# Attention output projection of head pairs: seven products of half blocks in place of eight, summed over the heads in SBUF

## Chip, core and metric

The kernel runs on one core of one Trainium2 chip. The metric is the device time of the whole program in microseconds (us), as the median of several runs. A profile is one further execution, recorded by the hardware; its span goes from the first to the last instruction.

## What is computed

One pre-norm transformer block on x of 1 x 1024 x 512, all in f32: x + attention(layernorm(x)), then that plus a feed-forward part of its own layernorm. The feed-forward part has three 512 x 512 matrices of signs and two ReLUs. The attention has 32 heads of 128 (keys) and 128 (values):

```python
q = einsum('bsd,de->bse', hidden, wq).reshape(B, S, H, DQ)[..., :DN]
k, v = ...                      # from hidden @ wkv, per head 128 and 128
scores = einsum('bqhd,bkhd->bhqk', q, k) * DQ ** -0.5      # causal mask
attn = einsum('bhqk,bkhd->bqhd', softmax(scores), v).reshape(B, S, H * DV)
return einsum('bse,ed->bsd', attn, wo)                     # wo: 4096 x 512
```

The change concerns the last line, the output projection: 1024 tokens x 4096 by 4096 x 512, summed over all heads.

## The kernel before, in words

Heads go in 16 pairs (G = 2). At the start x is loaded as eight tiles of 128 tokens (L76 to 79), normalised, and transposed into `xnT` (4 chunks of 128 features x 1024 tokens, L201).

**Projections q, k, v of a pair** (`products`, L260) are already done by a Strassen scheme: the operands are cut in two along the features, the two heads and the two token halves, and seven products are formed in place of eight. `token_sums` (L215) makes the token-side sums once; `weight_sums` (L227) makes four weight-side sums of 128 x 256 for each projection and pair, on GpSimd. The function yields after each product, so that the loop below can mix products with other work.

**The loop** (L441) walks over 32 heads x 8 tiles of 128 queries: 16 steps a pair, `s` = 0 to 15. A step issues

- the loads and weight sums due at this step (weights of the next pair),
- `probabilities` of the next step (L354): the score matmul into the only score buffer (`ps_sc`, two banks of PSUM), VectorE's mask-and-minimum (L369), ScalarE's exponential (L380), VectorE's reciprocal (L384), ScalarE's scaling (L385), and a VectorE transpose in blocks of 32 x 32 into `tb` (L387),
- one or two products of the chain v of this pair, q and k of the next one,
- at eight of the steps, `o_unit` (L342) of the *previous* pair: the output projection of one tile of 128 tokens, two matmuls of 512 columns (one for each head) into one PSUM bank, and a VectorE add of that bank to the tile of x (L352),
- after each fourth tile of queries, `exchange` (L391): 16 or 32 DMAs of 64 KB on SyncE's queue (SP), which finish the transposition from `tb` into `pT`,
- four steps after an exchange, `attend` (L407): probabilities times values for 512 queries, and a VectorE copy into `attnT` (L423).

A bank of PSUM takes one tile of 128 x 512 here; `ps_mm` has three banks, shared by the attention outputs and the projection, and `ps_st` three for the chain.

**The order of the work.** The program text gives the order in which instructions come up; when the program is built, a planner lays down a fixed order for each engine and each queue, in text order among the instructions whose inputs and buffers it expects to be there. On the chip each engine runs its list in order and waits where it must. A tile name with `bufs=n` has n buffers that are reused in turn.

**The end.** After the loop the last attend runs (L480), then for each tile of tokens the last pair's `o_unit` (L506), the second layernorm, a transposition, and a split into a coarse and a fine part. Three layers of matmuls follow (L520 twice, L545), and the final add takes the tile of x again (L553). The sign matrices are loaded in the last head's first step (L471) into buffers of weights that are free by then (L160).

Of the kernel before, what the change touches and what calls it, by code (L numbers as in the profile page):

```python
# [13 lines left out]
P = 128  # L14
# [5 lines left out]
G = 2  # L20
# [9 lines left out]
def kernel(  # L30
# [44 lines left out]
    xs = []  # L75
    for t in range(NT):  # L76
        xt = const.tile([P, D], F32, tag=f"x{t}", name=f"x{t}")
        nc.sync.dma_start(xt, x_v[:, t, :])
        xs.append(xt)
# [30 lines left out]
    def load_qk_weights(which, g):  # L110
        w = pairs.tile([P, G, NC, DN], F32, tag="wraw", name=f"w{'qk'[which]}{g}", bufs=3)
# [9 lines left out]
    def load_v_weights(g):  # L121
        wv_sb[g] = pairs.tile([P, NC, G * DV], F32, tag="wv", name=f"wv{g}")
        first = H * DN + g * G * DV
        nc.sync.dma_start(wv_sb[g], wkv_v[:, :, first : first + G * DV])
# [7 lines left out]
    load_v_weights(0)  # L132
    load_qk_weights(0, 1)
    load_o_weights(0)
# [25 lines left out]
    def sign_weights(i, k, slots):  # L160
# [4 lines left out]
        chunks = []  # L165
        for c in range(NC):
            if c % 2 == 0:
                pl, tag = slots[c // 2]
                w = pl.tile(
                    [P, 2, D], F32R, tag=tag, name=f"w{i}_{c}", bufs=3 if tag == "wraw" else None  # L170
                )
# [6 lines left out]
            nc.gpsimd.tensor_scalar(w[:, c % 2, :], kt[:, c, :], mul, add, ALU.mult, ALU.add)  # L178
            chunks.append(w[:, c % 2, :])
        return chunks  # L180

    def normalise(t, name):
        stats = small.tile([P, 6], F32, tag="stats", name=f"stats_{name}{t}")
        nc.vector.bn_stats(stats, xs[t])
# [7 lines left out]
        nc.vector.tensor_scalar(xn, xs[t], mv[:, 0:1], rstd, ALU.subtract, ALU.mult)  # L192
# [9 lines left out]
    for t in range(NT):  # L202
        nc.scalar.copy(xnT[:, :, t * P : (t + 1) * P], transposed(t, normalise(t, "a"), "a"))
# [22 lines left out]

    def weight_sums(which, g):  # L227
        s = pairs.tile([P, 4, 2, DN], F32, tag="wsum", name=f"wsum{'qkv'[which]}{g}")

        def A_(i, j):  # L230
            return A(which, g, i, j)

        nc.gpsimd.tensor_tensor(s[:, 0], A_(1, 0), A_(1, 1), ALU.add)  # L233
        nc.gpsimd.tensor_tensor(s[:, 1], s[:, 0], A_(0, 0), ALU.subtract)
        nc.gpsimd.tensor_tensor(s[:, 2], A_(0, 0), A_(1, 0), ALU.subtract)
        nc.gpsimd.tensor_tensor(s[:, 3], A_(0, 1), s[:, 1], ALU.subtract)
        w_sum[which, g] = s

    qT, kT, vs, attnT = {}, {}, {}, {}
# [20 lines left out]
    def products(which, g):  # L260
# [5 lines left out]
        if which == 2:  # L266
            d = []
            for h in (g * G, g * G + 1):
                vs[h] = heads.tile([P, NT, DV], F32, tag="v", name=f"v{h}")
                d.append([vs[h][:, k * TPB : (k + 1) * TPB, :] for k in range(NQB)])  # L270
# [49 lines left out]
        product(Y, s[:, 1], T[1], True, False)  # L320
# [6 lines left out]
        product(Y, s[:, 2], T[2], False, False)  # L327
# [4 lines left out]
        product(Z, s[:, 0], T[0], True, False)  # L332
# [5 lines left out]
        product(Z, s[:, 3], B(1, 1), False, True)  # L338
        plus(d[0][1], Z, u2)
        yield  # L340

    def o_unit(g, t):  # L342
        ps = ps_mm.tile([P, D], F32, tag="mm", name=f"ps_o{g}_{t}")
        for j in range(G):
            nc.tensor.matmul(  # L345
                ps,
                lhsT=attnT[g * G + j][:, t * P : (t + 1) * P],
# [59 lines left out]
    def attend(h, qb, pieces):  # L407
        g, j = divmod(h, G)
        if qb == 0:
            attnT[h] = heads.tile([P, S], F32, tag="attnT", name=f"attnT{h}")  # L410
# [11 lines left out]
        dst = attnT[h][:, qb * QB : (qb + 1) * QB]  # L422
        nc.vector.tensor_copy(dst.rearrange("p (t a i) -> p a t i", a=NB, i=B32), ps)  # L423

# [16 lines left out]
    for i, (h, qt) in enumerate(steps):  # L441
        g, j = divmod(h, G)
        s = NT * j + qt
        if s == 0:
            if g > 0:
                load_o_weights(g)
# [4 lines left out]
        if s == 5 and g + 1 < NG:  # L451
            weight_sums(1, g + 1)
            load_v_weights(g + 1)
# [9 lines left out]
        o_steps = (2, 4, 6, 8, 10, 12, 14, 15)  # L463
# [131 lines left out]
```

## Time and profile before

| what | value |
|---|---|
| median of 3 runs (lowest, highest) | 1413.53 us (1410.81, 1413.58) |
| the profiled execution's own time | 1412.72 us |
| its span | 1410.9 us |
| granted TensorE clock, mean | 0.989 |
| busy: TensorE matmul, VectorE, ScalarE, GpSimd | 1372.4, 733.1, 490.0, 153.8 us |
| output projection, matmul records (L345) | 512, busy 240.9 us |
| its VectorE adds (L352) | 128, 87.8 us busy, 686 ns each |
| DMAs of the exchange (L400) | 1536, median 2.0 us from issue to landing |

A matmul of f32 appears as two records and two weight loads in the profile, so 512 records are 256 matmuls. A group of instructions is shown as line, engine, operation, output<-input, shape, count, then its busy time, the mean of one, and the engine's idle time before them with what ended it. "Idle before" is time in which that engine waited for its next instruction's inputs; on an engine that is not the bottleneck it costs nothing. The chain of work is followed back from the last instruction to what released each piece. In a timeline each row has start, length, engine, line, operation, and in brackets the idle time before it.

### The profile page before, as it was taken

To read this page: it belongs to the slowest core of one execution; us is meant where nothing else is said; L and a number is where in the kernel's file an instruction comes from. 1 tells how busy PE (TensorE), PEld (TensorE's weight loads), DVE (VectorE), ACT (ScalarE), POOL (GpSimd) and SP (SyncE) were. 2 spreads that over 40 slices of the span, in tenths; PEclk is the share of its full clock that TensorE was granted. 3 is DMA by queue.
4 is the path that set the end of the run, shared out by engine and by line. 5 is a ranking of instruction groups with operands and counts; after the bars stand their busy time and mean duration, and the time that the engine had idled before them with its cause. 6 is when DMAs were issued, how large, how long until landed. Compare 5 with 4: busy or idle time off the path is not lost.

```text
span 1410.9 us, 15526 instructions
## 1 busy us (share of the span) xinstructions
PE 1372.4 (97%) x5000; PEld 791.6 (56%) x5000; DVE 733.1 (52%) x1561; ACT 490.0 (35%) x919; POOL 153.8 (11%) x213
## 2 busy tenths in 40 slices
PE   7999999999999999999999999999999999998598
PEld 4656464655646465554646455464645556463257
DVE  3455455555555555555455555544555554454275
ACT  2434333333333333333433333333333333333131
POOL 5110001010010101001010100100010110000200
PEclk9999999999999999999999999999999999998799
DMA  5234435353543435354443435344353434333401
GB/s 179 60 88 100 100 72 131 82 127 82 131 99 99 114 74 126 84 127 102 105 105 78 125 86 124 96 114 101 81 127 83 125 88 119 88 88 93 108 6 60
DMA packets 272176, 140.30 MB, mean 99 GB/s; under 512 B 26848, under 2 KB 265952, under 8 KB 272096
## 3 DMA queue, kind: packets, MB, share of 16 engines
q1 hardware_dynamic: 272096, 139.31, 39.7%
q8 instruction: 41, 0.67, 0.2%
q14 instruction: 39, 0.32, 0.1%
HBM read 36.44 MB, written 2.10 MB: 27 GB/s over the span
## 4 chain that ended last, share of the span: by engine, by line
PE 96%; DVE 2%; SPq 1%; DMA 1%; ACT 0%; issue 0%; DVEq 0%
PE sc L359 18%; PE ps_av L415 18%; PE ps_o L345 15%; PE Y_v L299 6%; PE Y_q L289 5%; PE Y_k L289 5%; PE X_v L299 4%; PE Z_v L299 4%; PE X_k L289 4%; PE X_q L289 4%; PE Z_k L289 4%; PE Z_q L289 4%; PE ps_h L520 2%; PE ps_out L545 1%; PE ps_q L255 1%; PE ps_k L255 1%
## 5 line engine op out<-in xcount | busy, mean ns | idle before, releaser
L380 ACT ACTIVATE p<-p,nmax 128x128 f32<-128x128 f32 (+7 forms) x256 | 198.0, 773 | 633.0 <-DVE nmax L369 625.8
L359 PE MATMUL sc<-kT,qT 128*128 128x512 f32 (+3 forms) x768 | 296.6, 491 | 7.0 <-DVE nmax L369 7.0
L415 PE MATMUL ps_av<-pT,v 128*128 128x512 f32 (+3 forms) x768 | 270.0, 495 | 14.6 <-DMA pT<-tb 14.6
L369 DVE CUSTOM_DVE_ANT_0 p<-sc,mask 128x128 f32<-128x128 f32 (+7 forms) x256 | 192.3, 751 | 153.6 <-PE sc L359 153.3
L345 PE MATMUL ps_o<-wo,attnT 128*128 128x512 f32 x512 | 240.9, 593 | 0.0
L415 PEld LDWEIGHTS ps_av<-pT,v 128*128 128x128 f32 x768 | 147.1, 194 | 150.1 <-issue 126.6
L359 PEld LDWEIGHTS sc<-kT,qT 128*128 128x128 f32 x768 | 140.4, 191 | 157.7 <-issue 142.9
L385 ACT ACTIVATE p<-p,rtotal 128x128 f32<-128x128 f32 (+7 forms) x256 | 194.5, 770 | 74.4 <-DVE rtotal L384 74.3
L387 DVE STREAM_TRANSPOSE tb<-p 128x128 f32<-128x128 f32 (+7 forms) x256 | 183.8, 755 | 12.3 <-ACT p L385 8.8
L352 DVE TENSOR_TENSOR x<-x,ps_o 128x512 f32<-128x512 f32 x128 | 87.8, 686 | 121.4 <-PE ps_o L345 121.2
L345 PEld LDWEIGHTS ps_o<-wo,attnT 128*128 128x128 f32 x512 | 92.1, 190 | 90.1 <-issue 87.8
L384 DVE RECIPROCAL rtotal<-total 128x1 f32<-128x1 f32 x256 | 40.5, 159 | 132.6 <-ACT p L380 132.5
L423 DVE COPY attnT<-ps_av 128x512 f32<-128x512 f32 x64 | 43.8, 684 | 55.2 <-PE ps_av L415 55.2
L233 POOL TENSOR_TENSOR wsumk<-wk 128x256 f32<-128x256 f32 x15 | 10.9, 726 | 491.6 <-DMA wk<-in_L_attn_wkv_dram 441.4
L299 PE MATMUL X_v<-wv,xnT 128*128 128x128 f32 x512 | 63.2, 275 | 0.0
L299 PEld LDWEIGHTS X_v<-wv,xnT 128*128 128x128 f32 x512 | 61.4, 192 | 1.3 <-issue 0.5
L289 PE MATMUL X_k<-xnT,wk 128*128 128x512 f32 x120 | 57.1, 592 | 0.0
L289 PE MATMUL X_q<-xnT,wq 128*128 128x512 f32 x120 | 57.1, 592 | 0.0
L233 POOL TENSOR_TENSOR wsumq<-wq 128x256 f32<-128x256 f32 x15 | 10.9, 726 | 339.1 <-PE Z_k L289 312.3
L380 ACT ACTIVATION_READ_ACCUMULATOR p<-p,nmax 128x1 f32 x256 | 47.8, 187 | 0.0
L312 DVE TENSOR_TENSOR v<-Z_v,u_v 128x512 f32<-128x512 f32 x32 | 22.1, 692 | 49.4 <-PE Z_v L299 49.4
L312 DVE TENSOR_TENSOR kT<-Z_k,u_k 128x512 f32<-128x512 f32 x30 | 20.6, 688 | 33.9 <-PE Z_k L289 33.9
(118 smaller groups left out, 1347.6 us busy)
## 6 DMA issues: line engine op xcount, KB each, us to landing
pT<-tb SPq DMA_DIRECT2D x1536, 64.0 KB, 2.0
wq<-in_L_attn_wq_dram SPq DMA_DIRECT2D x32, 256.0 KB, 3.3
wk<-in_L_attn_wkv_dram SPq DMA_DIRECT2D x32, 256.0 KB, 4.4
wv<-in_L_attn_wkv_dram SPq DMA_DIRECT2D x16, 512.0 KB, 4.1
wo<-in_L_attn_wo_dram SPq DMA_DIRECT2D x16, 512.0 KB, 4.0
x<-_attn_hidden_states_dram SPq DMA_DIRECT2D x8, 256.0 KB, 5.1
out_dram<-osb SPq DMA_DIRECT2D x8, 256.0 KB, 2.0
k<-in_L_ffn_k_dram SPq DMA_DIRECT2D x3, 256.0 KB, 3.4
```

The source lines that it names most:

```text
L289: nc.tensor.matmul(ps, lhsT=a[:, c, :], rhs=b[:, c, :], start=start, stop=stop, skip_group_check=True,)
L299: nc.tensor.matmul(ps[:, t, :], lhsT=b[:, c, t * P : (t + 1) * P], rhs=a[:, c, :], start=start and t == 0, stop=stop and t == TPB - 1, ski ...
L312: nc.vector.tensor_tensor(out, ps, other, ALU.add)
L345: nc.tensor.matmul(ps, lhsT=attnT[g * G + j][:, t * P : (t + 1) * P], rhs=wo_sb[g][:, j, :], start=(j == 0), stop=(j == G - 1),)
L352: nc.vector.tensor_tensor(xs[t], xs[t], ps, ALU.add)
L359: nc.tensor.matmul(sc[:, cols], lhsT=qT[h][:, qt * P : (qt + 1) * P], rhs=kT[h][:, cols], start=True, stop=True,)
L369: nc.vector.tensor_tensor_reduce(out=p[:, :n], in0=sc[:, :n], in1=mask[:, S - n :], scale=1.0, scalar=BIG, op0=ALU.add, op1=ALU.min, accum ...
L380: nc.scalar.activation(p[:, :n], p[:, :n], AF.Exp, bias=nmax, scale=-1.0, accum_out=total)
L385: nc.scalar.activation(p[:, :n], p[:, :n], AF.Copy, scale=rtotal)
L387: nc.vector.transpose(tb[qb][:, : qt + 1, :, i, :], p[:, :n].rearrange("p (c b k) -> p c b k", b=NB, k=B32))
L415: nc.tensor.matmul(ps[:, :, first:, :], lhsT=vs[h][:, kc, :], rhs=pieces[kc // TPB][:, kc % TPB, :, first:, :], start=(kc == 0), stop=(kc ...
L423: nc.vector.tensor_copy(dst.rearrange("p (t a i) -> p a t i", a=NB, i=B32), ps)
```

## The change

For each pair of heads, take the attention output as a 2 x 2 block matrix (two halves of 512 tokens by two heads) and wo's 256 rows as one (two heads by two halves of 256 output columns). The same scheme of seven products then gives the projection of a pair; each product is 512 tokens x 128 by 128 x 256, four matmuls of 256 columns.

- `o_products` (new) forms them. Each product is done in two halves of two token tiles, so that a half fills one PSUM bank; VectorE adds the half to `acc`, a tile of 7 x 4 x 256 per partition that keeps each *product* summed over the pairs (a copy for the first pair). The loop takes one half in every step from 2 to 15.
- `sums_of` (new) makes the weight-side sums on GpSimd, now in three new tiles and one in place, for q, k, v and wo alike. `attn_sums` (new) makes the four sums of attention outputs on GpSimd, one after the even head's second block and three after the odd head's.
- `add_products` (new) runs once, after the loop: eleven VectorE adds of 128 x 1024 combine the seven sums into x.
- The last pair keeps `o_unit`.
- To make room, x is loaded into the tile that becomes `acc`, and loaded again near the end into that of `xnT`. The weights of q and k have 2 buffers for 3, those of v 1 for 2, v itself 3 for 4; the attention outputs have one tile for each head of a pair and each half of the tokens. The load of wo goes from step 0 to step 6. The sign matrices and the hidden layers use other buffers.

The diff, cut to its core:

```diff
+    x_in = load_x("acc", "x_in")
...
     load_v_weights(0)
+    load_o_weights(0)
     load_qk_weights(0, 1)
-    load_o_weights(0)
...
+    def sums_of(a, tag, name, bufs):
+        t = pairs.tile([P, 3] + list(a(0, 0).shape[1:]), F32, tag=tag, name=name, bufs=bufs)
+        nc.gpsimd.tensor_tensor(t[:, 0], a(1, 0), a(1, 1), ALU.add)
+        nc.gpsimd.tensor_tensor(t[:, 1], t[:, 0], a(0, 0), ALU.subtract)
+        nc.gpsimd.tensor_tensor(t[:, 2], a(0, 1), t[:, 1], ALU.subtract)
+        nc.gpsimd.tensor_tensor(a(1, 0), a(0, 0), a(1, 0), ALU.subtract)
+        return [t[:, 0], t[:, 1], a(1, 0), t[:, 2]]
...
+    def attn_sums(g, early):
...
+        if early:
+            t0 = new(0)
+            nc.gpsimd.tensor_tensor(t0, b(0, 1), b(0, 0), ALU.subtract)
+            a_sum[g] = [t0]
+            return
+        t0, t1, t3 = a_sum[g][0], new(1), new(3)
+        nc.gpsimd.tensor_tensor(b(0, 1), b(1, 1), b(0, 1), ALU.subtract)
+        nc.gpsimd.tensor_tensor(t1, b(1, 1), t0, ALU.subtract)
+        nc.gpsimd.tensor_tensor(t3, b(1, 0), t1, ALU.subtract)
+        a_sum[g] = [t0, t1, b(0, 1), t3]
...
+        for m, left, right in (
+            (0, lambda: attn[g * G, 0], a(0, 0)),
+            (1, lambda: attn[g * G + 1, 0], a(0, 1)),
+            (2, lambda: a_sum[g][2], s[2]),
+            (3, lambda: a_sum[g][0], s[0]),
+            (4, lambda: a_sum[g][1], s[1]),
+            (5, lambda: a_sum[g][3], a(1, 1)),
+            (6, lambda: attn[g * G + 1, 1], s[3]),
+        ):
+            left = left()
+            for half in range(2):
+                ps = ps_mm.tile([P, 2, DH], F32, tag="mm", name=f"ps_o{g}_{m}_{half}")
+                for i in range(2):
+                    tok = slice((2 * half + i) * P, (2 * half + i + 1) * P)
+                    nc.tensor.matmul(
+                        ps[:, i, :], lhsT=left[:, tok], rhs=right, start=True, stop=True
+                    )
+                dst = acc[:, m, 2 * half : 2 * half + 2, :]
+                if g == 0:
+                    nc.vector.tensor_copy(dst, ps)
+                else:
+                    nc.vector.tensor_tensor(dst, dst, ps, ALU.add)
+                yield
...
+    def add_products(xt):
+        def to(d, k, m):
+            dst = xt[:, k * TPB : (k + 1) * TPB, d * DH : (d + 1) * DH]
+            nc.vector.tensor_tensor(dst, dst, acc[:, m], ALU.add)
+        def into(m, other):
+            nc.vector.tensor_tensor(acc[:, m], acc[:, m], acc[:, other], ALU.add)
+        to(0, 0, 0)
+        to(0, 0, 1)
+        into(4, 0)
+        into(2, 4)
+        into(5, 2)
+        to(1, 0, 5)
+        into(2, 3)
+        to(1, 1, 2)
+        into(4, 3)
+        into(6, 4)
+        to(0, 1, 6)
...
-            if g > 0:
-                load_o_weights(g)
...
+        if s == 2 and g > 0:
+            o_chain = o_products(g - 1)
+        if s == 5:
+            if g + 1 < NG:
+                weight_sums(1, g + 1)
+                load_v_weights(g + 1)
+            else:
+                x_out = load_x("xnT", "x_out")
+                xs = [x_out[:, t, :] for t in range(NT)]
+        if s == 6 and g > 0:
+            load_o_weights(g)
...
-        o_steps = (2, 4, 6, 8, 10, 12, 14, 15)
-        if g > 0 and s in o_steps:
-            o_unit(g - 1, o_steps.index(s))
...
         if i in to_attend:
             attend(*to_attend.pop(i))
+        if g > 0 and s >= 2:
+            next(o_chain, None)
...
+    add_products(x_out)
     for i in sorted(to_attend):
         attend(*to_attend[i])
```

## The prediction, made before the changed kernel was run

> **What bounds the kernel now.** I read the engines' shares first, then the chain of work that ended last, then stretches of time, then the groups, then the DMA queue. The page's engine line and the three rows of the slices that matter:
>
> ```profile
> PE 1372.4 (97%) x5000; PEld 791.6 (56%) x5000; DVE 733.1 (52%) x1561; ACT 490.0 (35%) x919; POOL 153.8 (11%) x213
> ...
> PE   7999999999999999999999999999999999998598
> ...
> PEclk9999999999999999999999999999999999998799
> ...
> PE 96%; DVE 2%; SPq 1%; DMA 1%; ACT 0%; issue 0%; DVEq 0%
> ```
>
> TensorE has work in 97% of the span and is 96% of the chain; only around slice 36 and after it does it lack work. The busy times of four stretches, three pairs of heads in the middle and the last pair:
>
> ```profile
> 593.11:674.46 81.35, 81.35 (x298) 46.23 (x298) 43.13 (x92) 28.68 (x55) 8.48 (x12) 1.00 0.42 104
> 674.46:755.82 81.36, 81.36 (x299) 46.27 (x298) 43.09 (x92) 28.68 (x55) 8.47 (x12) 1.00 0.43 104
> 1162.64:1243.91 81.27, 81.27 (x298) 46.21 (x298) 42.93 (x92) 28.80 (x55) 5.66 (x8) 1.00 0.40 98
> 1243.91:1331.83 87.92, 66.33 (x244) 38.64 (x244) 38.48 (x82) 28.12 (x50) 7.36 (x12) 0.88 0.41 100
> ```
>
> The columns are length, PE, PEld, DVE, ACT, POOL, clock, DMA share, GB/s. A pair takes 81.36 us and TensorE is busy in all of it: there a microsecond of matmul taken away is a microsecond of the span. In the last pair TensorE has 66 of 88 us, and something else sets the pace. So the change is priced in two stages.
>
> **What a record costs.** A matmul of f32 stands as two records. The chain between 1240 and 1244 us (start, length, work) has four widths side by side:
>
> ```profile
> 1240.68 1.72 PE ps_o L345 x4
> 1242.40 0.22 PE sc L359 x2
> ...
> 1243.48 0.43 PE sc L359 x2
> ```
>
> Four records of 512 columns take 1.72 us; the two of 1242.40 are 128 columns wide (0.11 us each), the two of 1243.48 are 256 wide (0.215 us each). Over the trace, from one record's start to the next, the means are 429.5 ns (512 columns, L345), 215.9 ns (256, L359) and 111.6 ns (128, L299). A record thus costs its columns and about 3 ns more, and the loads of its stationary operand are hidden even at 128 columns, where each record has a load of its own.
>
> **The products, term by term.** Before, a pair of heads has 8 x 2 matmuls of 512 columns: 32 x 429.5 ns = 13.74 us. After, 7 products x 4 token tiles = 28 matmuls of 256 columns: 56 x 215.9 ns = 12.09 us. That is 1.65 us less in each pair. Bounds: the 256-column record costs at least half of 512 (214.8 ns) and at most two of 128 (223.2 ns), so 1.25 to 1.72 us. The sums for 15 pairs run beside the next pair; the last pair's (L506) keeps its form. 14 of the 15 lie in full stretches: 14 x 1.65 = 23.2 us. The fifteenth lies in the last pair, where only the work up to 1276 us is dense: three old units (3 x 1.72 = 5.16 us) give way there to five half products (5 x 0.86 = 4.3 us), 0.8 us less.
>
> A rule speaks against this. The Trainium skill, "TensorE: Matmul & The Clock Gate", section "Back-to-back issue gap", says that in a real stream of loads and matmuls the spacing falls far less than the width does: about 81 ns at 128 columns against 131 ns at 512. On a straight line that makes 256 columns cost 98/131 = 0.75 of 512, and the pair would rise from 13.7 to 18.0 us, an estimate of +64 us over 15 pairs. The trace's ratio is 215.9/429.5 = 0.503, so the row decides.
>
> **VectorE** evacuates 14 halves of 128x512 where it evacuated 8 tiles; L352 takes 686 ns, so +6 x 0.686 = 4.1 us a pair, 43.1 to 47.2 us of a new period of 79.7 (59%). It is in order, and what queues behind an add is the mask-and-minimum of a score tile (L369), which frees the only score bank for the next score matmul. I took the time from the end of L369 to the next score matmul in the middle pairs: at 13 of the 16 steps it is 0.9 us or more on average (up to 5.8), at the three around a pair's start 0.50, 0.84 and 0.17 us. Six added adds fall on those three of 16 steps 6 x 3/16 = 1.1 times a pair, and each takes 0.69 less some 0.5 us of slack: 1.1 x 0.19 = 0.21 us, 14 x 0.21 = 2.9 us. Bounds: nothing, since the planner lays each engine's order out afresh, to 4.1 us a pair, if every added add is passed on. I take 2.9, near the lower end, because the page's waits give PE only 7 us for this reason in the whole run:
>
> ```profile
> PE sc L359 <- DVE nmax L369: 7.0, 6, 2.1
> ```
>
> **GpSimd.** Each pair gets 4 sums of wo (128x256, 0.73 us by L233) and 4 of attention outputs (128x512: between 0.73 and the 2.35 us of L216 at 1024 elements; 1.27 us on a straight line): 8.0 us on 8.5, in 79.7. Busy time is no issue; order may be. The third product needs a sum that GpSimd makes after the copy (L423) of the odd head's second block. In the middle pairs that copy is 35 us into the next pair (627.96 from 593.11), and step 6, where the product stands, begins about 31 us in: it is late by 4 us and a sum. What waits is a product that TensorE may take later, with 45 us of pair left for the 10 remaining halves (8.6 us). Left on the path: nothing, to 1.27 us a pair if the planner prices the sum at nothing; I take nothing. GpSimd's own waits at the next operand sums (up to 35 us, for wk) stand before the copy, and the next, for the q products, some 11 us after it.
>
> **Buffers.** wraw 3 to 2, wv 2 to 1, v 4 to 3, attention outputs to one of each: each reload now follows the last reader by at least one step in the program. SP runs a steady pair as 96 issues of about 0.64 us and six of weights: 65 of 81 us, so over 14 us of room remain at 79.7. The wo load goes from step 0 to step 6, past 16 exchange issues, at 0.59 us, and is wanted 50 us later. The second wq waits at the start for the q products (30.6 us) and is wanted near 70 us; behind it on SP stands the second wk, wanted at about 95 us, then the exchange at 55 us. Each: nothing.
>
> **The end.** Added: the input again (8 issues in 3.80 us at the start, L78), 14 - 8 adds, and 11 adds of 1024 elements. The nearest rows are 1.21 us (L369 at 1024) and two of 0.69 us: 11 x 1.21 = 13.3 us. SP and VectorE in the last pair:
>
> ```profile
> 1267.68 36.94 SPq L400 DMA_DIRECT2D pT<-tb  x48
> 1304.72 1.67 SPq L164 DMA_DIRECT2D k<-in_L_ffn_k_dram  x3
> 1306.49 34.87 SPq L400 DMA_DIRECT2D pT<-tb  x48
> ```
> ```profile
> 1339.93 0.69 DVE L352 TENSOR_TENSOR x<-x,ps_o 128x512 f32<-128x512 f32 x1 [16.07 <-PE ps_o L345]
> ```
>
> From 1267.7 us on the exchange's issues pace the stage. The input's 8 stand ahead of the first 48, in which SP still waits 6.0 us for a transpose, so 3.8 us fit. The 11 adds need the last half product (about 1324 us) only for two of them; VectorE is idle for 16 us before 1339.93, and 13.3 us fit. Without that cover they cost 3.8 + 13.3 = 17.1 us; if the earlier ones fill holes they may even do without it. I take nothing.
>
> **Sum.** 23.2 + 0.8 - 2.9 = 21.1 us. The profiled execution took 1412.7 us (span 1410.9), so 1391.6; the median of the runs, 1413.5, is 0.8 above it: 1392.4, and 1392 is my number.
>
> **Rivals.** (a) The end isn't hidden: input and adds run into the last exchange or after it, +17.1 us: 1409. For it: the stage is SP's and nothing but a hole covers the adds; against: 16 us of idle VectorE at the right place. (b) Score matmuls and third products wait in each pair, 0.3 to 1.3 us: 14 x 0.8 = 11 us more, 1403. For it: steps with 0.17 us of slack; against: 60% load. (c) Slower: VectorE's queue at the score bank. Every added add is passed on in full to the next score matmul, 6 x 0.686 = 4.1 us a pair, 14 x (4.1 - 1.65) = 34 us: 1448. It decides from 0.28 us per added add (1.65/6). For it: one score bank, and an in-order queue in which an add also holds for its product (1.03 us at L352 in the timeline); against: 0.9 us of slack and more at 13 steps. (d) It doesn't save: a 256-column record at 245 ns (13.74/56) takes it all, 1413. Against: 118 records at 215.9 ns.
>
> **How the numbers follow.** Forecast 0.63, (a) 0.12, (b) 0.12, (c) 0.09, (d) 0.04. Full gain without stalls is 1412.7 - 15 x 1.72 = 1387, and a shorter last stage may give 2 us more: the range starts at 1385. It ends at 1409 and takes in (a) and (b); (c) and (d) are left out. A difference of 0.2% (2.8 us) is what a measurement of this kernel can tell: faster 0.87, same 0.04, slower 0.09.
>
> **What would show it.** PE's records go from 5000 to 5360 (840 of 256 columns, 32 of 512 left); the 256-column ones stand 216 ns apart; a middle pair takes 79.7 us with PE busy in all of it; VectorE 47 us and GpSimd 16.5 us of it; the 11 adds lie before the first add of L352's last eight. A PE wait for VectorE or GpSimd in every pair shows (b) or (c); a gap of over 10 us more between the last exchange and the first ps_h shows (a).

## The result, and the profile after

| | before | after |
|---|---|---|
| median of 4 runs each, on one chip | 1413.05 us | 1424.64 us |
| lowest, highest | 1410.81, 1413.58 | 1422.80, 1426.02 |
| the profiled execution, its span | 1412.72, 1410.9 us | 1423.88, 1422.1 us |

The ratio is 1.0084, with a 95% interval of 1.0067 to 1.0102: the changed kernel is slower by 0.8%, where I had forecast 1.5% faster (1392 us, at most 1409). The page's engine line, the slices and the chain's shares, of the kernel after:

```profile
PE 1360.6 (96%) x5360; PEld 857.9 (60%) x5360; DVE 796.1 (56%) x1662; ACT 491.2 (35%) x919; POOL 275.6 (19%) x333
...
PE   7999999999999999999999999999999999997498
...
PEclk9999999999999999999999999999999999999799
...
PE 87%; SPq 5%; DVE 4%; DMA 2%; POOL 1%; issue 1%; ACT 0%; DVEq 0%
```

Looked at from so far off, nothing seems wrong: TensorE has 12 us less to do, as forecast in kind, and is still "96% busy". The slices hide what happened, because a slice of 36 us with 1 us of waiting is still a 9. The chain tells more: TensorE's share fell from 96 to 87%, and GpSimd is in it for the first time. Two middle pairs and the last pair up to the last exchange (columns as before):

```profile
266.87:348.95 82.08, 82.08 (x337) 52.39 (x335) 46.60 (x98) 28.69 (x55) 16.27 (x20) 1.00 0.41 103
761.17:843.44 82.27, 80.71 (x322) 50.67 (x320) 46.30 (x98) 28.82 (x55) 16.36 (x20) 1.00 0.41 103
1254.29:1351.60 97.31, 66.97 (x212) 38.73 (x213) 55.87 (x103) 29.25 (x52) 18.05 (x20) 0.89 0.47 120
```

The later pair takes 82.27 us where it took 81.36, and TensorE is idle in 1.56 of them by this view; the earlier one is dense, but holds 337 records where the later one has 322. These are the two places where the saving went. "Busy" still flatters: it contains gaps of about 0.1 us between records. So I counted differently from here on. **Work** is the sum of all records, each at the spacing measured in the prediction (111.6, 215.9, 429.5 ns for 128, 256, 512 columns); **idle** is what is left of the time. For the 14 pairs before the last one and after the first:

| kernel | length of the 14 pairs | work | idle | last pair: first score to first ps_h |
|---|---|---|---|---|
| before | 1136.7 us | 1135.8 | 0.9 | 120.2 |
| after | 1148.6 | 1121.5 | 27.0 | 118.6 |

The account closes. Had only the 14 x 1.65 = 23.2 us gone, work would stand at 1112.6. It stands 8.9 us higher: products of later pairs are formed ahead of time in the first six of these pairs (the 15 extra records above, mostly v products of 128 columns). The last pair has that much less to do (72.6 us of matmul up to the first ps_h for 83.2), but is only 1.6 us shorter; experiment 8 shows, on a mended order, what it waits for. And idle rose by 26.1. So the last pair starts 11.9 us later by the pairs and 0.2 by the start; it is 1.6 us shorter, what follows 0.6 longer: 11.1 of the 11.2 us between the spans.

**Where TensorE is idle.** The first row of TensorE's waits before the last pair (1 to 1254 us; us in total, times, longest):

```profile
PE ps_o L389 <- POOL attn L361: 14.1, 9, 1.6
```

The rows below it belong to the start and stood there before. This one is new, and it comes once in each of the last nine of these pairs. Its place in one pair, in the timelines of VectorE, GpSimd and TensorE:

```profile
712.64 2.70 DVE L467 STREAM_TRANSPOSE tb<-p 128x640 f32<-128x640 f32 x3
715.26 0.65 DVE L502 COPY attn<-ps_av 128x512 f32<-128x512 f32 x1
```
```profile
715.99 1.27 POOL L361 TENSOR_TENSOR attn<-attn,attn 128x512 f32<-128x512 f32 x1 [5.75 <-DVE attn L502]
```
```profile
711.71 2.32 PE L494 MATMUL ps_av<-pT,v 128*128 128x512 f32 x8
713.87 1.88 PE L289 MATMUL X_k<-xnT,wk 128*128 128x512 f32 x4
717.31 1.13 PE L389 MATMUL ps_o<-wo,attn 128*128 128x256 f32 x4 [1.56 <-POOL attn L361]
718.28 0.39 PE L439 MATMUL sc<-kT,qT 128*128 128x128 f32 x2
```

Read from the bottom up: the third product (m = 2) stands in TensorE's list four records behind the odd head's second attend. The attend ends at 713.87, and its copy would be done by 714.5. But VectorE has three transposes ahead of the copy, so it starts at 715.26 and ends at 715.9; GpSimd then takes 1.27 us for the sum, and the four records of X_k are over at 715.6. TensorE stands still for 1.7 us, and the next score matmul, behind the product in the list, with it.

### The profile page after: what moved, and what is told of

It reads as the page before. It is cut to its first block, busy times and chain, and to the rows that moved or that the text cites. A ratio compares the mean times of both kernels' runs of the same rounds, so it can differ in the third digit from the quotient of the medians.

```text
span 1422.1 us, 16625 instructions
## 1 busy us (share of the span) xinstructions
PE 1360.6 (96%) x5360; PEld 857.9 (60%) x5360; DVE 796.1 (56%) x1662; ACT 491.2 (35%) x919; POOL 275.6 (19%) x333
## 4 chain that ended last, share of the span: by engine, by line
PE 87%; SPq 5%; DVE 4%; DMA 2%; POOL 1%; issue 1%; ACT 0%; DVEq 0%
PE sc L439 16%; PE ps_av L494 15%; PE ps_o L389 11%; PE Y_v L299 6%; PE Y_k L289 5%; PE Y_q L289 5%; SPq L480 5%; PE X_v L299 4%; PE Z_v L299 4%; PE X_q L289 4%; PE Z_k L289 4%; PE Z_q L289 3%; PE X_k L289 3%; PE ps_h L617 2%; DVE tb L467 2%; DMA pT<-tb 1%
## 5 line engine op out<-in xcount | busy, mean ns | idle before, releaser
L439 PE MATMUL sc<-kT,qT 128*128 128x512 f32 (+3 forms) x768 | 297.2, 495 | 11.1 <-DVE nmax L449 11.1
L396 DVE TENSOR_TENSOR acc<-acc,ps_o 128x512 f32<-128x512 f32 x196 | 131.7, 681 | 153.0 <-PE ps_o L389 151.7
L389 PE MATMUL ps_o<-wo,attn 128*128 128x256 f32 x360 | 92.4, 390 | 14.1 <-POOL attn L361 14.1
L389 PEld LDWEIGHTS ps_o<-wo,attn 128*128 128x128 f32 x360 | 65.8, 192 | 43.4 <-POOL attn L361 24.3
L502 DVE COPY attn<-ps_av 128x512 f32<-128x512 f32 x64 | 43.8, 684 | 65.9 <-PE ps_av L494 65.9
L389 PE MATMUL ps_o<-osum,at 128*128 128x256 f32 x240 | 56.7, 380 | 0.0
L389 PEld LDWEIGHTS ps_o<-osum,at 128*128 128x128 f32 x240 | 45.7, 190 | 12.5 <-issue 7.2
L317 ACT ACTIVATE p_k<-X_k 128x512 f32<-128x512 f32 x15 | 8.9, 593 | 115.2 <-PE X_k L289 115.2
```

The source lines that it names most:

```text
L389: nc.tensor.matmul(ps[:, i, :], lhsT=left[:, tok], rhs=right, start=True, stop=True)
L396: nc.vector.tensor_tensor(dst, dst, ps, ALU.add)
L439: nc.tensor.matmul(sc[:, cols], lhsT=qT[h][:, qt * P : (qt + 1) * P], rhs=kT[h][:, cols], start=True, stop=True,)
```

## The experiments

Each round names its theories by letters, which hold for that round alone; its text says what a letter means. Ratios are against the kernel before, run on the same chip.

**1. The waiting product later.** The product that needs no late sum goes first: in the list of `o_products`, m = 3 (whose sum is formed half a pair earlier) stands ahead of m = 2.

```diff
-            (2, lambda: a_sum[g][2], s[2]),
             (3, lambda: a_sum[g][0], s[0]),
+            (2, lambda: a_sum[g][2], s[2]),
```

> Only the order of the products is changed: 0, 1, 3, 2, 4, 5, 6, so that the third one formed needs only the early sum. Theory S (TensorE waits for the sum of attention outputs on GpSimd, which stands behind the copy of the odd head's second block): the 1.7 us wait in each middle pair goes, the idle time of a middle pair falls from 2.6 to about 0.9 us, and the time falls by 15 to 19 us to 1406 to 1410 us. Rival P (the heads are paced by another loop of 82.3 us, through SP's exchange or VectorE, and the wait only shows it): the period stays at 82.3 us, the idle time turns up elsewhere, 1422 to 1427 us.

1415.87 us, ratio 1.0017 (1.0008 to 1.0027). The wait is gone and 9 us of the loss with it, but not the whole: 1406 to 1410 was expected, and the idle time of a middle pair fell to 1.46 us, not to 0.9. A middle pair, and in it the place of the former wait, TensorE and then VectorE:

```profile
756.50:837.60 81.10, 80.63 (x322) 50.51 (x321) 46.08 (x98) 28.76 (x55) 16.36 (x21) 1.00 0.41 104
```
```profile
705.84 1.03 PE L389 MATMUL ps_o<-osum,at 128*128 128x256 f32 x4
...
712.29 1.02 PE L289 MATMUL Y_k<-T,wsumk 128*128 128x512 f32 x2
713.93 0.46 PE L439 MATMUL sc<-kT,qT 128*128 128x128 f32 x2 [0.61 <-DVE nmax L449]
```
```profile
709.36 2.70 DVE L467 STREAM_TRANSPOSE tb<-p 128x640 f32<-128x640 f32 x3
711.98 0.65 DVE L502 COPY attn<-ps_av 128x512 f32<-128x512 f32 x1
712.56 1.21 DVE L449 CUSTOM_DVE_ANT_0 p<-sc,mask 128x1024 f32<-128x1024 f32 x1
```

A pair is now 81.10 us, only 0.26 less than before the change, with 79.64 us of work in it. The next wait has come up: a new head's first score needs the score bank, whose mask-and-minimum stands on VectorE behind the same three transposes and the copy. In the kernel before, that score came 1.4 us or more after its mask-and-minimum had ended (rows in experiment 7).

**2. Without the sums of attention outputs.** The third to sixth product read attention outputs in place of their sums; GpSimd's four operations a pair are left out, and the output isn't the reference's. The order of products is the one after the change.

```diff
-        if qb == 1 and g + 1 < NG:
-            attn_sums(g, early=(j == 0))
...
-            (2, lambda: a_sum[g][2], s[2]),
+            (2, lambda: attn[g * G, 1], s[2]),
```

> The sums of attention outputs are left out, and the products that need them take attention outputs as they are, so the output is another; all matmuls, adds and sums of wo stay. Theory S: no product waits for GpSimd; a middle pair falls to 79.7 to 80.6 us and the time to 1398 to 1410 us. Rival P: a middle pair stays at 82 us, 1420 us or more.

1417.3 us, 1.0033 (1.0020 to 1.0046), middle pairs of 81.10 us with 1.46 us idle, the same as in 1 and again short of what was expected. Two different edits that take away the same wait give the same pair: the wait for the sum is shown as one cause, of 1.2 us a pair (82.27 to 81.10), not of the 1.7 that it lasts.

**3. The half products ahead of exchange and attend in a step.** Only the place in the loop's text changes.

```diff
+        if g > 0 and s >= 2:
+            next(o_chain, None)
         if qt % TPB == TPB - 1:
...
             attend(*to_attend.pop(i))
-        if g > 0 and s >= 2:
-            next(o_chain, None)
```

> The half product of a step is issued ahead of the exchange and the attend of that step, where the old unit stood, and not behind them. Theory S: the wait for the third product's sum may stay (1.7 us a pair), but the halves no longer stand in bursts behind the probabilities-times-values, so the short gaps of 0.1 us at score matmuls and halves (0.9 us a pair) shrink; 1410 to 1422 us. Rival P: no change, 1422 to 1427 us.

1416.98 us, 1.0032 (1.0019 to 1.0045). Pairs of 81.82 us: the wait for the sum stays (1.60 us for 1.73 by the spacings), but idle falls from 2.62 to 2.18. In the kernel after, halves follow an attend in bursts of three, and the weight load of the third (PEld) waits for the VectorE add that frees its bank:

```profile
624.19 0.73 PEld L389 LDWEIGHTS ps_o<-wo,attn 128*128 128x128 f32 x4 [0.32 <-DVE acc L396]
```

TensorE stands still for 0.18 us there. Such gaps come twice in a middle pair of the kernel after and once here; the rest of the fall is 0.13 us of the wait and small gaps at scores.

**4. Edits 1 and 3 together.**

> The order 0, 1, 3, 2 and the half product ahead of the exchange and the attend, with no hold on the v products. Theory H with S: no wait for the sum, products of the next pair at hand as filler: a middle pair of 79.6 us of matmuls and 0.4 to 1 us of waits, the first six pairs still 81 to 82 us: 1403 to 1410 us. If the waits at the scores come back as with the hold (1.8 us): 1414 to 1418 us.

1411.65 us, 1.0001 (0.9991 to 1.0011): 13 us better than the kernel as changed, and level with the one before. A middle pair:

```profile
1000.34:1081.27 80.93, 80.46 (x322) 50.61 (x321) 46.17 (x98) 28.54 (x55) 16.33 (x21) 1.00 0.42 105
```

0.43 us less than before the change, where the products save 1.65. Of the 4 us by which this kernel is ahead of experiment 1, the 14 pairs give 1.0 (1137.5 for 1138.5 us) and the last pair 4.0 (117.6 for 121.6): there SP's waits for transposes fall from 2.9 to 0.4 us. The place of the halves pays at the end more than in the pairs.

**5. The memory plan alone.** The kernel before, old projection, with the changed buffers and places of loads (weights of q and k in two, of v in one, v in three, attention outputs by head and half, wo's load at step 6).

```diff
-        w = pairs.tile([P, G, NC, DN], F32, tag="wraw", name=f"w{'qk'[which]}{g}", bufs=3)
+        w = pairs.tile([P, G, NC, DN], F32, tag="wraw", name=f"w{'qk'[which]}{g}")
...
+        if s == 6 and g > 0:
+            load_o_weights(g)
```

> The kernel before with the memory plan of the changed one only (wraw 2, wv 1, v 3, one tile for each block of the attention outputs, wo loaded at step 6, the order of the first loads); the projection stays as it was, and the tiles that the last stage takes are new ones. Theory S: the smaller number of buffers costs nothing, 1411 to 1416 us and a middle pair of 81.4 us without idle time. Rival M (the buffers hold the weights or the heads up): a middle pair of 82 us or more, 1420 to 1426 us.

1415.88 us, 1.0025 (1.0015 to 1.0034): it costs some 3 us without any new product. The pairs are dense but longer, as work of later pairs comes into earlier ones (1138.9 us of work in the 14 pairs for 1135.8) and idle is 3.9 for 0.9. The last pair gives 2.5 us of it back.

**6. Products held back.** So that v products can't be formed ahead, the load of the next pair's v weights goes to step 12 and their sum to step 13; alone, with edit 1, and with edits 1 and 3. A fourth kernel has the second load of the input on ScalarE's queue besides; a fifth holds back only to steps 10 and 12.

```diff
-                load_v_weights(g + 1)
...
+        if s == 12 and g + 1 < NG:
+            load_v_weights(g + 1)
+        if s == 13 and g + 1 < NG:
+            weight_sums(2, g + 1)
```

> The changed kernel with one edit: the v weights of the next pair are loaded at step 12 (for 5) and summed at step 13 (for 10), so that its v products can't be formed ahead. Theory H (TensorE's saved time went into products formed ahead of their pair, 9.9 us by the start of the last pair, where it is not the bound and the time is lost): the pairs 2 to 6 hold 79.6 us of matmuls as the later ones do, not 80.5 to 81.4; but they then also wait as the later ones do (2.6 us a pair for 0.9), so 9.9 us less and 5 x 1.7 = 8.5 us more, 1421 to 1425 us, with the last pair starting at 1248 to 1256 us. Rival T (the last pair takes back what is moved into it): 1430 us or more.

> The same hold on the v products, with the order of products 0, 1, 3, 2, 4, 5, 6. Theory H: against the order alone (1415.9 us) 9.9 us less and 5 x 0.75 = 3.8 us more of waits in the pairs 2 to 6: 1408 to 1412 us. Rival T: 1416 us or more.

> The hold, the order 0, 1, 3, 2, and the half product issued ahead of the exchange and the attend of its step. Theory H with S: a middle pair of 79.6 us of matmuls and 0.5 to 1 us of waits, 80.1 to 80.7 us, from the second pair on; 1398 to 1405 us, faster than both kernels. Rival T: the last pair grows by 8 to 10 us and the time is 1408 to 1414 us.

> As the one before, and the second load of the input is issued from ScalarE's queue, not from SP's. Theory Q (in the last pair SP's issues are on the chain, 3.87 us of them for the input): 3 to 4.5 us less than the one before. Rival: SP has waits there in which the 8 issues fit, no difference over 1 us.

> As the one before, with the v weights of the next pair loaded at step 10 and summed at step 12, so that about 2 us of its products are at hand as filler at a pair's start. Theory H: some of both, a middle pair of 80 to 81 us from the fourth pair on: 1404 to 1411 us. If filler is short at the scores: 1414 to 1418 us.

| kernel | median, ratio (interval) | a middle pair: length, idle | 14 pairs: work, idle |
|---|---|---|---|
| hold alone | 1419.48, 1.0055 (1.0035 to 1.0075) | 81.87, 2.23 | 1112.5, 29.7 |
| with edit 1 | 1421.05, 1.0066 (1.0048 to 1.0084) | 81.87, 2.23 | |
| with edits 1 and 3 | 1416.59, 1.0035 (1.0022 to 1.0049) | 81.47, 1.83 | 1113.4, 25.0 |
| the same, input on ScalarE's queue | 1416.73, 1.0038 (1.0026 to 1.0051) | 81.47, 1.83 | |
| edits 1 and 3, held to steps 10 and 12 | 1424.43, 1.0087 (1.0072 to 1.0102) | 82.01, 2.36 | |

My theory that the work formed ahead is the loss fell here. Held back, work is 1112.5 us, the forecast 1112.6 almost to the tenth, and what the work lost, idle mostly gained, now at the first scores of a pair (0.95 and 0.69 us at the second and third score with edits 1 and 3, 1.64 us at the first in the last row's kernel). Alone the hold gains some 4 us on the kernel after; on top of edit 1, or of 1 and 3, it loses 5. With 1 and 3, 4.1 of these lie in the last pair (121.7 us for 117.6), which now forms its 112 records of v products itself, where it had 20 left. So what is formed ahead does come back in the last pair, and the time of a pair follows neither the work nor any one wait.

**7. The saving alone.** The kernel before, with two of the 16 projection matmuls of each pair left out (so the output lacks them) and nothing added anywhere: 4 records of 512 columns, 1.72 us a pair, 25.8 us over 15 pairs.

```diff
-        for j in range(G):
+        n_heads = 1 if t % 4 == 0 and g + 1 < NG else G
+        for j in range(n_heads):
```

> The kernel before with two of the 16 projection matmuls of a pair left out (the second head of tiles 0 and 4; the output is another), and nothing added: 1.72 us of matmuls less in each of 15 pairs. If TensorE sets the pace, as the prediction had it, 23 to 26 us less: 1387 to 1390 us. Theory H (the order of the plan forms later products ahead and the last pair doesn't take the time back; score matmuls wait once nothing is left to form ahead): the pairs up to the ninth keep 81 us, about 10 us are lost in this way, and later pairs fall to 79.7 to 81 us: 1396 to 1406 us.

1398.51 us, 0.9902 (0.9887 to 0.9917): 13.5 us of the 25.8. An early and a later pair:

```profile
508.31:590.49 82.18, 82.12 (x313) 47.45 (x312) 43.07 (x93) 29.28 (x56) 8.46 (x12) 1.00 0.41 103
753.30:834.05 80.75, 80.28 (x293) 45.58 (x292) 42.56 (x92) 28.76 (x55) 8.46 (x12) 1.00 0.43 105
```

This is the run that settles it. The early pair has 20 records more than the later one and is longer than the 81.36 us of before; the later one gains 0.61 us for 1.72 taken out, and has a 0.5 us wait for VectorE at the odd head's first score, with not one added VectorE or GpSimd operation in the kernel. The mask-and-minimum that frees the bank and that score, in the same pair of the kernel before and of this one:

```profile
790.77 1.22 DVE L369 CUSTOM_DVE_ANT_0 p<-sc,mask 128x1024 f32<-128x1024 f32 x1
793.40 0.38 PE L359 MATMUL sc<-kT,qT 128*128 128x128 f32 x2
```
```profile
789.89 1.21 DVE L370 CUSTOM_DVE_ANT_0 p<-sc,mask 128x1024 f32<-128x1024 f32 x1
791.26 0.46 PE L360 MATMUL sc<-kT,qT 128*128 128x128 f32 x2 [0.47 <-DVE nmax L370]
```

Both pairs start at 753.3 us. The score stands 2.1 us earlier in the new order, VectorE's operation only 0.9, and the 1.4 us of room between them is gone.

By the spacings, the 14 pairs hold 14.3 us less work (not 24.1, as some of the last pair's products are formed in them) and 9.3 us more idle: 5.0 us shorter. The last pair has 11.5 us less work and is 7.5 us shorter (112.7 for 120.2), and 1.0 comes behind it. So the time is theory H's, but not its mechanism: the last pair does take back much of what is formed ahead. The largest loss is the idle time in the pairs.

**8. The end.** On the kernel of experiment 4, first: the second load of the input as one DMA for eight; no eleven adds of `add_products` (the output lacks the projection of 15 pairs); both; and the eight loads issued at step 13 in place of 5.

```diff
-                x_out = load_x("xnT", "x_out")
+                x_out = const.tile([P, NT, D], F32, tag="xnT", name="x_out")
+                nc.sync.dma_start(x_out, x_v)
...
-    add_products(x_out)
```

> The best order so far (first-half sums' product ahead of the waiting one, half products ahead of exchange and attend; 1411.65 us) with the second load of the input as one DMA in place of eight. In that kernel the eight issues take 3.88 us of SP in the last pair, between the 96 and the 48 exchange issues. Theory R (SP's issues pace the last pair, so the reload is paid in full): 3.4 us less, 1408.2, and the last pair to the first ps_h shorter by as much. Theory V (the end is long because VectorE's adds hold the last softmax steps): no change, 1411.7. Theory N (neither; what is lost is lost in the pairs): no change here and within 1 us without the adds too.

> The same kernel without the eleven adds that combine the seven sums (the projection of 15 pairs is missing from the output; the products and their adds to the sums stay). Theory V: the adds, 11 x 1.2 = 13.3 us of VectorE in the last pair, delay transposes and with them the exchange: 3 to 5 us less, 1407 to 1409. Theory R and theory N: within 1 us of 1411.7.

> Both: one DMA for the input and no eleven adds (the projection of 15 pairs is missing from the output). It bounds what the added end costs in all. Theory R: 1408.2; theory V: 1407 to 1409; if both hold, 1404 to 1405; theory N: within 1 us of 1411.7. The kernel before with two matmuls a pair left out had 112.7 us from the last pair's first score to the first ps_h, this order 117.6: if the added end is the whole difference, 112.7 to 113 here.

> The same kernel (with its adds) with the eight loads of the input issued eight steps later, behind the first half of the last head's steps, in place of between the exchanges of the even head. Theory R: no better than 1411.7, as the issues stand before the last 32 or 16 exchange DMAs just the same, or 1408 if SP waits there anyway for the last transposes. Theory V: the adds then wait for the input and fall later, 3 to 8 us more, 1415 to 1420. Theory N: 1411.7.

Against experiment 4 nothing moved by more than some 2 us, and I took theory N for shown. But SP's queue in the first of them speaks against it:

```profile
1278.88 0.54 SPq L538 DMA_DIRECT2D x_out<-_attn_hidden_states_dram  x1
1279.52 0.56 SPq L132 DMA_DIRECT2D wo<-in_L_attn_wo_dram  x1
1280.18 8.51 SPq L480 DMA_DIRECT2D pT<-tb  x7
```

Seven issues of 0.64 us don't take 8.5 us. In the trace these DMAs tell of their landing by eight semaphores in all, given out in turn, and each issue waits until the DMA that last had its semaphore has landed; here that is the DMA eight places before it.

The load lands 9.2 us after its issue, at 1288.1, and the seventh exchange issue, eight places behind it, goes out at 1288.10. The load hadn't been taken from SP's path at all. Hence two more, in which GpSimd fills the tile with zeros and no load is there (the input is missing from the last sum and the second layernorm), with and without the adds:

```diff
-                x_out = load_x("xnT", "x_out")
+                x_out = const.tile([P, NT, D], F32, tag="xnT", name="x_out")
+                for t in range(NT):
+                    nc.gpsimd.memset(x_out[:, t, :], 0.0)
```

> The best order so far (1411.65 us) without the second load of the input: GpSimd, which is idle there, fills the tile with zeros instead (the input is missing from the last sum and from what the second layernorm sees; all else stays). With one DMA for eight, SP's next exchange issue waited 3.7 us for that load to land, so the load had not really been taken from SP. Theory R (the reload is paid, by issues or by that wait): 3.9 us less, 1407.5 to 1408.5, and 113.5 to 114 us from the last pair's first score to the first ps_h, which makes up most of the distance to the 112.7 of the kernel with two matmuls a pair left out. Theory N (SP waits for the softmax there anyway): 1411 to 1412, and 117 to 118 us.

> The same, also without the eleven adds of the seven sums (the projection of 15 pairs is missing too). Theory R with free adds: as without the load alone, 1407.5 to 1408.5. If the adds are paid as soon as the load no longer is: 1404 to 1406, and 112 to 113 us in the last pair. Theory N: 1411 to 1412.

| kernel | median | ratio (interval) | last exchange issued | first score to first ps_h |
|---|---|---|---|---|
| experiment 4: load and adds | 1411.65 | 1.0001 (0.9991 to 1.0011) | 1340.1 | 117.6 |
| one DMA | 1412.89 | 0.9999 (0.9990 to 1.0008) | 1340.4 | 119.7 |
| load, no adds | 1413.31 | 1.0003 (0.9994 to 1.0013) | 1341.2 | 120.1 |
| one DMA, no adds | 1411.39 | 0.9985 (0.9976 to 0.9994) | 1339.1 | 116.9 |
| eight loads later | 1411.23 | 0.9988 (0.9979 to 0.9998) | 1340.5 | 117.7 |
| adds, no load | 1412.01 | 0.9998 (0.9989 to 1.0008) | 1340.4 | 117.4 |
| neither | 1406.00 | 0.9954 (0.9940 to 0.9969) | 1334.0 | 113.1 |

The exchange's column is the end of its last issue. Taking out one of the two brings nothing, taking out both some 6 us: **each covers the other**. In the profiles, 4.3 us of the 6 stand in the last pair (117.4 to 113.1 with the adds taken out as well); the start up to the second pair, which differs by up to 2 us from one profile to another, has 1.6 more. VectorE without the load, then SP's wait in that kernel, then VectorE with neither, then VectorE with the load and no adds:

```profile
1308.60 3.17 DVE L407 TENSOR_TENSOR acc<-acc 128x1024 f32<-128x1024 f32 x2
1311.69 2.69 DVE L467 STREAM_TRANSPOSE tb<-p 128x640 f32<-128x640 f32 x3
```
```profile
SPq L480 <- DVE tb L467: 5.6, 1, 5.6
```
```profile
1305.07 2.69 DVE L467 STREAM_TRANSPOSE tb<-p 128x640 f32<-128x640 f32 x3
```
```profile
1309.44 2.70 DVE L467 STREAM_TRANSPOSE tb<-p 128x640 f32<-128x640 f32 x3 [2.76 <-DMA pT<-tb]
```

The adds stand ahead of three transposes on VectorE and make them 5.0 us later, counted from the last pair's first score (1243.82 us without the load, 1242.21 with neither), and SP waits 5.6 us for them. With the load in place, SP comes to the exchange behind them some 6 us later anyway (1308.10 us in experiment 4, 1302.73 without the load), and the wait is gone from its list (0.4 us): the same time is lost to the load. With the load and no adds, it is the transposes that wait, 2.76 us, until the exchange that the load held up has emptied their tile. The 113.1 us of the kernel with neither are close to the 112.7 of experiment 7, so the end is nearly the whole of that difference, and it is also what kept the last pair of this kernel from gaining by the work formed ahead.

Last, a full kernel in which both are moved behind the softmax: the load on ScalarE's queue behind the last probabilities, the adds into the input after it, the other six on GpSimd.

```diff
-            nc.vector.tensor_tensor(acc[:, m], acc[:, m], acc[:, other], ALU.add)
+            nc.gpsimd.tensor_tensor(acc[:, m], acc[:, m], acc[:, other], ALU.add)
...
+    nc.scalar.activation(x_out[:, :, 0], last_p[0][:, :NT], AF.Copy, scale=last_p[1])
+    for t in range(NT):
+        nc.scalar.dma_start(x_out[:, t, :], x_v[:, t, :])
```

> A full kernel: the best order so far (1411.65 us) with the added end moved behind the softmax. The second load of the input is issued on ScalarE's queue after the last probabilities (a small ScalarE write of last probabilities into the tile, overwritten by the load, makes it wait for them), so SP has no reload and the five VectorE adds into the input come after the last transpose; the six adds among the sums go to GpSimd. Theory E (load and adds each cover the other, and the end costs 6 us, as the run without both says: 1406.0): 1405.5 to 1407, 0.9950 to 0.9960 of the kernel before, 113 to 114 us from the last pair's first score to the first ps_h. Theory N (it was something else in that run, such as the missing input itself): 1411 to 1412. If the adds, now late, reach into the last pair's projection behind the last attend: 1408 to 1415.

1410.9 us, 0.9987 (0.9978 to 0.9996): a miss, and a telling one. The transposes come as early as with neither, but SP waits for the load although it isn't in its queue. SP's waits of this kernel, and its chain:

```profile
SPq L483 <- DMA x_out<-_attn_hidden_states_dram: 5.7, 2, 5.1
```
```profile
1312.36 4.24 DMA x_out<-_attn_hidden_states_dram
1316.62 4.51 DMA x_out<-_attn_hidden_states_dram
1321.15 0.58 SPq L483
```

In the trace both queues use the same eight semaphores, so the exchange's issue that takes a load's semaphore next waits for that load, whichever queue it went out from; here ScalarE's own issues wait in the same way, and 8 of them take 6.4 us. It fits that ScalarE's queue brought nothing in experiment 6 (SP waits 2.9 us for the load there). This kernel and the one with the loads later are ahead of the kernel before by some 0.12%, under the 0.2% that I had set for telling a difference.

## Why the prediction was wrong, point by point

- **What a record costs: right.** Records went from 5000 to 5360, and those of 256 columns stand 215.8 to 216.1 ns apart. With the products held back (experiment 6) the work of the 14 pairs fell by 23.3 us, for 23.2 forecast. The Trainium skill's spacings ("TensorE: Matmul & The Clock Gate", "Back-to-back issue gap"), by which the change would have cost an estimated 64 us, don't hold for these records.
- **GpSimd: the step that failed first.** "Left on the path: nothing, to 1.27 us a pair if the planner prices the sum at nothing; I take nothing." I had worked out myself that the product is "late by 4 us and a sum". The fault is the next sentence, that it "waits" as "a product that TensorE may take later". TensorE takes its list in order: later products aren't late, the whole list behind the product is. It was up to 1.7 us of standing still in nine pairs, over my upper bound, because VectorE's three transposes ahead of the copy came on top of the sum; worth 9 us of the total (experiment 1). The place of the halves behind each attend costs 4 more, nearly all of it in the last pair (experiment 4).
- **VectorE: a small term, but not for its reason.** 2.9 us taken, and none measured: no wait of TensorE for it lies in the pairs before the last. That this fits is luck, as it was hidden behind the other wait: with that gone, 4.0 us of the waits between 1 and 1243 us are for the mask-and-minimum (experiment 1), though the row that causes them is three transposes and a copy, not the added adds, and experiment 7 has the wait without these.
- **Buffers: wrong by 3 us.** "Each: nothing." I asked of each buffer whether a reload comes in time, and not what order the planner makes when a load or a release moves. Experiment 5 has 3 us for it.
- **The end: wrong by 6 us.** "3.8 + 13.3 = 17.1 us ... I take nothing." Some 6 of them are paid on the kernel of experiment 4 (experiment 8); in the kernel after, they weren't measured by themselves. The cover was there, the 16 us hole of VectorE before the last eight adds, but the planner put the adds ahead of it, where their inputs were ready and the last transposes stood behind them; and I priced the load by its issues ("so 3.8 us fit"), not by the landing that the exchange waits for. Rival (a) had both in mind, at 17.1 us.
- **The sum: the step that failed most.** "...there a microsecond of matmul taken away is a microsecond of the span." 100% busy over a pair doesn't show by how much TensorE is the bound. Behind it stands the chain from one score through VectorE's queue to the next. I had its slack at each of the 16 steps, and used it for the price of added work alone; it also limits what removed work can bring. And the slack doesn't stay where it is: the smallest, 0.50, 0.84 and 0.17 us at a pair's first three scores, gave waits with products held back (experiment 6), but the wait of experiments 1, 4 and 7 is at the odd head's first score, which had 1.4 us or more before the planner moved it up. Experiment 7 measures the return: 13.5 of 25.8 us. At that rate, an estimate by proportion, the forecast's 24 us of matmul are worth some 12.6. With the order mended and the end taken out (experiment 8, neither) 6.9 of them are there; the memory plan's 3 us (experiment 5) may stand between, and the rest is open. From there the end (6), the place of the halves (4) and the wait (9) lead up to the 1424.6 measured; these are the steps between the runs.
- **The rivals.** (b), waits of score matmuls and third products, had the right mechanism, at 0.3 to 1.3 us a pair; 2.56 us more idle was measured in a later pair (2.62 against 0.06), so it ends on the slower side. (c), the slower one, foresaw the added adds as the cause, which no run shows. (a) came true for a third of its price, and not by the sign that I gave for it: from the last exchange issue to the first ps_h it is 21.4 us for 21.0 before, as the end is paid ahead of that issue. (d) didn't.

What stays open: why a pair doesn't go under about 80.8 us in any of these kernels when work is 79.6. 0.5 to 0.6 us of it is the wait at a head's first score; the rest are gaps of some 0.1 us, most of them at scores, whose cause wasn't isolated. All runs took the order that the planner laid down; whether another order of the same work would return more than 13.5 of 25.8 us wasn't tried. Nor was a full kernel tried that needs no second load at all.

## What to carry to other kernels

An engine that is busy all the time bounds the kernel only down to the next chain: before pricing a saving in full, leave some of the work out and time that, which would have halved this forecast. The slack of the next chain is a warning and no more, as the planner moves the work: 1.4 us of it became a wait of 0.5. In a fixed order, a result that comes late isn't "taken later": it stops everything behind it on that engine, so products with early inputs go ahead of those with late ones (13 us here, from moving two pieces of text). And where two suspects lie side by side, taking away one at a time clears both; the pair has to go together before either is let off.

## What the runs showed of the hardware

**VectorE and GpSimd hold each other up.** In the last pair the adds of two SBUF tiles meet GpSimd's preparation of the sign matrices. VectorE and GpSimd of the kernel after, then GpSimd of the kernel before:

```profile
1317.55 1.22 DVE L407 TENSOR_TENSOR acc<-acc 128x1024 f32<-128x1024 f32 x1
...
1324.55 1.62 DVE L407 TENSOR_TENSOR acc<-acc 128x1024 f32<-128x1024 f32 x1
...
1327.64 1.21 DVE L404 TENSOR_TENSOR x_out<-x_out,acc 128x1024 f32<-128x1024 f32 x1
```
```profile
1322.93 3.71 POOL L176 TENSOR_SCALAR w_signs<-k 128x512 fp32r<-128x512 uint8 x3
1326.64 2.77 POOL L176 TENSOR_SCALAR w_signs<-k,f_twice,f_minus 128x512 fp32r<-128x512 uint8 x1
```
```profile
1312.02 0.77 POOL L178 TENSOR_SCALAR w<-k,f_twice,f_minus 128x512 fp32r<-128x512 uint8 x1
```

The same add takes 1.22 us alone and 1.62 beside GpSimd's three operations of 1322.93; GpSimd's next takes 2.77 us for 0.77, and ends 0.6 us after the last of VectorE's adds (1328.85). The Trainium skill states an exclusive lock between adds with two SBUF inputs and GpSimd operations that read SBUF ("SBUF — State Buffer", "SBUF: two separate sides"); the numbers agree with it. What it cost in time wasn't separated from the adds themselves.

**The first two records after a wait stand further apart.** The four records of a half product that waited for the sum stand as 1.13 us (717.31 in the kernel after), those of one that didn't as 1.03 (705.84 in experiment 1). The second record starts 0.32 us after the first in place of 0.216, in all eight halves of the later pairs that waited over a microsecond. The same step also stands behind waits of 0.08 us (the third half of a burst, experiment 3) and at some scores without one, so what causes it isn't shown.
